# Attention scores computed twice, the second time with keys on partitions, and other products handed out between PSUM banks

## The chip, the cores and the metric

The kernel runs on one core of a Trainium2 chip. A core has five engines that each work through a queue of their own: TensorE (PE) for matrix products and transposes, VectorE (DVE), ScalarE (ACT) and GpSimd (POOL) for elementwise work, and SyncE (SP), which here issues the DMAs. The engines wait for one another through semaphores. The metric is the device time of one execution in microseconds (us). The kernel before took 1918.61 us as the median of 3 runs (1916.52 to 1922.07).

## What is computed

The input `x` is 4 sequences of 256 tokens with 512 channels in float32. Three layers follow one another: causal attention with an adapter, a feed-forward layer with clusters together with a state-space mixer, and the same feed-forward layer once more at the end. The change concerns the attention and the order in which the first feed-forward layer is worked off beside it. The part of the reference that matters:

```python
qkv = jnp.einsum('btc,oc->bto', x, w_attn)
q, k, v = jnp.split(qkv, 3, axis=-1)          # 32 heads of 16 channels, rotated
scores = jnp.einsum('bhqd,bhkd->bhqk', q, k) / jnp.sqrt(hd)
scores = jnp.where(causal, scores, -jnp.inf)
attn = jax.nn.softmax(scores, axis=-1)
y = jnp.einsum('bhqk,bhkd->bhqd', attn, v)
...
ascores = jnp.einsum('bhqd,xhkd->bhqk', q, ak) / jnp.sqrt(C)   # 10 adapter positions
ascores = gating[0] * jax.nn.softmax(ascores, axis=-1)
y = y + jnp.einsum('bhqk,xhkd->bhqd', ascores, av)
return jnp.einsum('btc,oc->bto', y, w_proj)
```

## The kernel before

The kernel is written for a framework that hands out tiles from pools and orders the instructions itself: each engine's queue is made by a list scheduler from the order in which the code asks for the work, from the dependences and from the buffers that a pool has. So the queues of PE, DVE, ACT, POOL and SP need not follow the source line by line; where this matters, the order of the built program is told. A pool with n buffers lets the n+1st tile begin only when the first has been read. PSUM, where PE writes, has eight banks; the attention's pools hold 2 (`ps`), 3 (`ps_s`), 2 (`ps_t`) and 1 (`ps_y`) of them.

Exact float32 products are made of three products of rounded parts (`mm3`, lines 106 to 114): high with high, high with low, low with high. A 512x512 projection of 128 tokens is 12 matmuls in this form.

Attention goes over 4 batches b, and in a batch over 8 units u of 4 heads. Two units share one set of turned pieces (q, 8 heads):

- `prepared(b)`: normalization, transposes, projections to queries, keys and values (`projected`), rotation on DVE and POOL.
- `pieces(b, q)`: a head's 16 channels are stacked as high, high, low parts and one slot of zeros, 64 rows in all (`stacked`: an ACT cast at L305, a POOL subtraction at L306), and turned by PE (`trp`, L380), so that one product over 64 rows gives an exact score. The first head of a pair lies in rows 0 to 63, the second in rows 64 to 127.
- `scores(b, u)`: queries on partitions. Score products (`sc`, L425), the causal mask added by a product with a constant (L429), the row maximum on DVE (L434), the exponential on ACT for each head with the row sum accumulated (L437).
- `turn`: the exponentials are transposed by PE (`ptr`, L452), three groups of four per unit, and copied from PSUM by DVE and ACT (L453).
- `weigh`: the product with the values (`py`, L462 and L468), four heads in the four 32-column groups. `gathered`: transposed back (`try`, L479), divided by the row sum (L484, L485).
- `adapter_scores` (`pa` L390, `sa` L394, `tra` L397), once per q; `adapted(b)`: the adapter's softmax for all heads at once (L496 to L503), then `pt`, `paT` and `pya`.
- `closed` adds both parts and turns them (L527, L530); `ended` projects them (`po`) and adds to x (L543).
- `fed`: the first feed-forward layer for 128 tokens (`Feed.tile`, 24 products of 288 columns). Four tiles may start when the last batch begins, the others when their attention has ended.

The loop (L608) runs over units; in one iteration it asks for the scores of unit i, the transposes of i-1, the product with the values of i-2 and the gathering of i-3. At its end it takes one step of each generator in `jobs` (the next batch's `prepared`, the adapter) and two of `slow` (`fed`). A step there is a whole projection of 12 products, or a whole feed-forward tile.

The mixer follows from about 392 us on. The change does not touch it.

Of the kernel before, what the change touches and what calls it, by code (L numbers as in the profile page):

```python
# [9 lines left out]
F32 = mybir.dt.float32  # L10
# [67 lines left out]
def hybrid_kernel(  # L78
# [36 lines left out]

    def warmed(o, vs):

        for v in vs:
            nc.tensor.matmul(o[:, : v.shape[1]], ones, v, start=True, stop=True)
# [52 lines left out]
    class Feed:  # L172
# [23 lines left out]
        def tile(self, t, xs, halves):  # L196

            p2 = self.p2
            pa, pb = halves
            for j, o in enumerate(halves):  # L200
                mm3(o, [[v[:, k, :] for v in xs] for k in range(KC)],
                    [[v[:, k, j, :] for v in self.w] for k in range(KC)])
# [29 lines left out]
    def attention(later):  # L232
        with ExitStack() as es:
# [6 lines left out]
            ps = pool("a_m", 2, space=PSUM)  # L240
            ps_s = pool("a_s", 3, space=PSUM)
            ps_t = pool("a_t", 2, space=PSUM)
# [25 lines left out]
            def projected(xs, w, where):  # L268
                pq = where[0].tile([P, C], F32, name="pq", tag=where[1])
                mm3(pq, [[v[:, k, :] for v in xs] for k in range(KC)],  # L270
                    [[v[:, k, :] for v in w] for k in range(KC)])
                return pq
# [20 lines left out]
            stacks = [[w1.tile([P, 8, 4, HD], F32R, name=f"st{f}{i}") for i in range(NS)] for f in range(2)]  # L293
            for f in range(2):
                for v in stacks[f]:
                    nc.gpsimd.memset(v.bitcast(F32), 0.0)
# [4 lines left out]
            def stacked(src, f, n=P):  # L301
                st = stacks[f][turn_at[f] % NS]
                turn_at[f] += 1
                v = src.unsqueeze(2)
                nc.scalar.copy(st[:n, :, HI[f], :], v.to_broadcast([n, 8, 2, HD]))  # L305
                nc.gpsimd.tensor_tensor(  # L306
                    st[:n, :, LO[f], :], src, st[:n, :, 0, :].bitcast(F32), ALU.subtract
                )
                return st.rearrange("p h s d -> p (h s d)")
# [9 lines left out]
            def adapter_weights():  # L319
# [9 lines left out]
                for q in range(4):  # L329
                    s = stacked(ak[:20, q * 8 : q * 8 + 8, :], 1, 20)  # L330
# [20 lines left out]
            vs = [w1.tile([P, 2, C + HD], F32, name=f"av{i}") for i in range(2)]  # L351
            for v in vs:
                nc.gpsimd.memset(v[:, :, C:], 0.0)

            qk, turned_ = {}, {}

            def prepared(b):
# [3 lines left out]
                for c in range(2):  # L361
                    xs.append(normed(norm, 2 * b + c))
                    yield
                    for f, w in ((0, wq_s), (1, wk_s)):
                        qk[b, c, f] = rotated(projected(xs[c], w, where), c, f, f"r{f}{c}")
                        yield
                for c in range(2):
                    nc.scalar.copy(vs[b % 2][:, c, :C], projected(xs[c], wv_s, where))
                    yield

            def pieces(b, q):

                out = []
                for f in range(2):
                    o = p2.tile([P, 4, L], F32R, name=f"pc{f}", tag=f"pc{f}")
                    for c in range(2):
# [5 lines left out]
                        nc.scalar.copy(o[:, :, cs], tr) if f else nc.vector.tensor_copy(o[:, :, cs], tr)  # L382
                    out.append(o)
                turned_[b, q] = out
# [17 lines left out]
            state = {}  # L402

            def begin(b):
                state[b] = {
                    "as": p2.tile([P, 2, NH, NA], F32, name="as"),
                    "rs": p2.tile([P, 2, NH], F32, name="rs"),
# [5 lines left out]
            def scores(b, u):  # L413

                qT, kT = turned_[b, u // 2]
                rs = state[b]["rs"]
                es_ = [p2.tile([P, 4, (c + 1) * P], F32, name=f"e{c}", tag=f"e{c}") for c in range(2)]
                for c in range(2):
                    n = (c + 1) * P
                    for pr in range(2):  # L420
                        rows = slice(64 * pr, 64 * pr + 64)
                        sc = ps_s.tile([P, 2, L], F32, name="sc", tag="sc")
                        for j in range(2):
                            blk = (u % 2) * 2 + j
                            nc.tensor.matmul(  # L425
                                sc[:, j, :], qT[rows, blk, c * P : (c + 1) * P], kT[rows, blk, :],
                                start=(j == 0), stop=False,
                            )
                        nc.tensor.matmul(  # L429
                            sc[:, :, n - P : n], identb, negb.unsqueeze(1).to_broadcast([P, 2, P]),  # L430
                            start=False, stop=True,
                        )
                        nm = p3.tile([P, 2], F32, name="nmx", tag="nmx")
                        nc.vector.tensor_reduce(nm, sc[:, :, :n], AX.X, ALU.max, negate=True)  # L434
                        for j in range(2):
                            h = 4 * u + 2 * j + pr
                            nc.scalar.activation(  # L437
                                es_[c][:, 2 * j + pr, :], sc[:, j, :n], AF.Exp,
                                bias=nm[:, j : j + 1], accum_out=rs[:, c, h : h + 1],
                            )  # L440
                return es_

            def turn(es_):
                e0, e1 = (
                    p2.tile([P, 4, (2 - c) * P], F32, name=f"eT{c}", tag=f"eT{c}") for c in range(2)
                )
                for src, k, dst in (
                    (es_[0], 0, e0[:, :, :P]), (es_[1], 0, e0[:, :, P:]), (es_[1], 1, e1)
                ):
                    pt = ps_t.tile([P, 4, P], F32, name="ptr", tag="pt")  # L450
                    for j in range(4):
                        nc.tensor.transpose(pt[:, j, :], src[:, j, k * P : (k + 1) * P], ident)  # L452
                    nc.scalar.copy(dst, pt) if k else nc.vector.tensor_copy(dst, pt)  # L453
                return e0, e1

            def weigh(b, u, eT):

                v = vs[b % 2]
                py = ps_y.tile([P, L], F32, name="py", tag="py")
                for j in range(4):  # L460
                    h = 4 * u + j
                    nc.tensor.matmul(  # L462
                        py[32 * j : 32 * j + 32, :], v[:, 0, h * HD : h * HD + 32], eT[0][:, j, :],
                        start=True, stop=False,
                    )
                for j in range(4):
                    h = 4 * u + j
                    nc.tensor.matmul(  # L468
                        py[32 * j : 32 * j + 32, P:], v[:, 1, h * HD : h * HD + 32], eT[1][:, j, :],
                        start=False, stop=True,  # L470
                    )
                ys = p2.tile([P, L], F32, name="ys")
                nc.scalar.copy(ys, py)
                return ys

            def gathered(b, u, ys):
                tr = ps.tile([P, 2, 4, 32], F32, name="try", tag="m")
                for c in range(2):
                    nc.tensor.transpose(  # L479
                        tr[:, c].rearrange("p h d -> p (h d)"), ys[:, c * P : (c + 1) * P], ident  # L480
                    )
                st = state[b]
                ry = p2.tile([P, 2, 4], F32, name="ry")
                nc.vector.reciprocal(ry, st["rs"][:, :, 4 * u : 4 * u + 4])  # L484
                nc.vector.tensor_tensor(  # L485
                    st["y"][:, :, 64 * u : 64 * u + 64].rearrange("p c (h d) -> p c h d", h=4),
                    tr[:, :, :, :HD], ry.unsqueeze(3).to_broadcast([P, 2, 4, HD]), ALU.mult,
# [45 lines left out]
            def ended(b):  # L533
                st = state.pop(b)
                pos = []
                for c in range(2):
                    pos.append(ps.tile([P, C], F32, name="po", tag="m"))
                    cs = slice(c * P, (c + 1) * P)
                    mm3(pos[c], [[v[:, k, cs] for v in st["yT"]] for k in range(KC)],
                        [[v[:, k, :] for v in wp_s] for k in range(KC)])  # L540
                for c, po in enumerate(pos):
                    t = 2 * b + c
# [3 lines left out]
                    if feed is None:  # L546
                        continue
                    feed.norm.stats(t)
                    feed.norm.root(t, t + 1)
                    if b < B - 1:  # L550
                        slow.append(fed(feed, t))
                    else:
                        late[t] = p2.tile([P, C], F32, name="axn", tag="t1")
                        feed.norm.scale(t, late[t])
# [6 lines left out]
            def fed(f, t):  # L561
                xs = normed(f.norm, t)
                yield
                f.tile(t, xs, [ps.tile([P, FH], F32, name="pd", tag="m") for _ in range(2)])
# [40 lines left out]
            n = B * 8  # L605
            es_, eTs, yss = {}, {}, {}
            feed, late = None, {}
            for i in range(n + 3):  # L608
                if i < n:
                    b, u = divmod(i, 8)  # L610
                    if u == 0:
                        begin(b)
                        pieces(b, 0)
                        if i == 0:
                            jobs.append(adapter())
                        if b + 1 < B:
                            jobs.append(prepared(b + 1))
                    if u == 6:
                        jobs.append(adapted(b))
                    es_[i] = scores(b, u)  # L620
                    if u % 2 == 0 and i > 0:
                        adapter_scores(b, u // 2)
                if 1 <= i <= n:
                    eTs[i - 1] = turn(es_.pop(i - 1))
                if 2 <= i <= n + 1:
# [584 lines left out]
```

## Time and profile before

| | before |
|---|---|
| median of 3 runs | 1918.61 us (1916.52 to 1922.07) |
| profiled execution, own time | 1916.66 us |
| its span, first to last instruction | 1914.9 us |
| PE busy | 1866.0 us, 97% |
| DVE, ACT, POOL busy | 77%, 72%, 19% |
| attention (with the first feed-forward mixed in) | about 0 to 392 us |
| first scores of batches 0, 1, 2, 3 | 36.06, 120.23, 202.3, 284.5 us |
| mean granted TensorE clock | 0.990 |

How to read a profile line: `L425 PE MATMUL sc<-pc,pc 64*128 64x256 f32 x128 | 32.7, 332 | 0.3 <-ACT e L437 0.3` is the group of matmuls from line 425 that write tiles named `sc` from two tiles named `pc`; the weights have 64 rows and 128 columns, the moving operand is 64x256. There are 128 of them, busy 32.7 us in all and 332 ns each on average, and PE sat idle for 0.3 us just before them, which an ACT instruction of line 437 ended. Matmuls are pipelined, so their records overlap: how long one really holds the engine is seen from start to start. In a timeline a line begins with the start and the duration in us. A table of stretches gives, after the stretch's length, the busy time and the number of instructions of PE, its weight loads, DVE, ACT and POOL, then the clock that TensorE was granted as a share of full speed, the DMA share and GB/s.

### The profile page before, as it was taken

The page shows a single profiled execution, that of the slowest core. Times are in us where ns is not written, and L with a number is a line of the kernel's source. Part 1 is how long each engine was busy: PE and PEld are TensorE (multiplying, and loading weights), DVE is VectorE, ACT ScalarE, POOL GpSimd, SP SyncE. Part 2 cuts the span into 40 slices and gives each one's busy share as a digit, 9 for nine tenths or more (in the row PEclk, how much of TensorE's full clock was granted, in tenths as well). Part 3 has the DMA queues.
Part 4 walks back from the last instruction along what each step waited for, and adds up shares of the span by engine and source line. Part 5 has one row for each costly group of instructions (what it writes and reads, how often), then busy time and mean ns, then how long its engine had stood idle before and what let it go on. Part 6 is the DMA issues. An engine that isn't in the chain of part 4 may idle for free.

```text
span 1914.9 us, 29954 instructions
## 1 busy us (share of the span) xinstructions
PE 1866.0 (97%) x10690; PEld 1468.9 (77%) x10690; DVE 1475.2 (77%) x2324; ACT 1383.2 (72%) x2873; POOL 361.0 (19%) x308
## 2 busy tenths in 40 slices
PE   7999999989999999999999999999999999999997
PEld 6767767767777787888787878877777788787786
DVE  5556657678998777877877797778777877877777
ACT  5665667557898677876787787778677877786753
POOL 4212120011331111222111121212111211131100
PEclk7999999989999999999999999999999999999999
DMA  4000000014455554544455454446454554455341
GB/s 141 1 1 1 1 21 24 12 38 155 169 192 184 160 168 140 160 154 160 149 164 161 149 172 156 148 147 187 149 165 154 160 159 160 138 166 162 119 123 49
DMA packets 151909, 240.35 MB, mean 126 GB/s; under 512 B 12368, under 2 KB 77520, under 8 KB 151760
## 3 DMA queue, kind: packets, MB, share of 16 engines
q1 hardware_dynamic: 151760, 238.44, 39.1%
q8 instruction: 84, 1.38, 0.3%
q14 instruction: 65, 0.53, 0.1%
HBM read 202.75 MB, written 35.65 MB: 124 GB/s over the span
## 4 chain that ended last, share of the span: by engine, by line
PE 84%; DVE 6%; ACT 4%; DMA 2%; issue 1%; SPq 0%; DVEq 0%; ACTq 0%
PE pp L112 12%; PE pp L113 11%; PE pp L114 11%; PE pyy L928 8%; PE pog L112 6%; PE pog L114 6%; PE pog L113 6%; PE sc L425 3%; PE trx L913 3%; PE ptr L452 2%; DVE acc L854 2%; PE py L462 1%; PE sc L429 1%; PE trp L380 1%; DMA wor<-in_wout_dram 1%
## 5 line engine op out<-in xcount | busy, mean ns | idle before, releaser
L112 PE MATMUL pp<-mx,w 128*128 128x512 f32 (+1 forms) x1160 | 465.6, 401 | 8.4 <-DVE acc L854 7.9
L114 PE MATMUL pp<-mx,w 128*128 128x512 f32 (+1 forms) x1160 | 454.2, 392 | 0.0
L113 PE MATMUL pp<-mx,w 128*128 128x512 f32 (+1 forms) x1160 | 454.2, 392 | 0.0
L854 DVE SCALAR_TENSOR_TENSOR acc<-pp,cw_s,acc 128x1012 f32<-128x1012 f32 (+2 forms) x240 | 304.8, 1270 | 23.1 <-ACT acc L847 22.4
L902 DVE TENSOR_TENSOR em<-em,gm 128x1536 f32<-128x1536 f32 x128 | 228.4, 1785 | 94.3 <-ACT em L896 86.0
L112 PEld LDWEIGHTS pp<-mx,w 128*128 128x128 f32 x1160 | 218.6, 188 | 66.0 <-issue 9.9
L114 PEld LDWEIGHTS pp<-mx,w 128*128 128x128 f32 x1160 | 218.5, 188 | 45.5 <-issue 0.4
L113 PEld LDWEIGHTS pp<-mx,w 128*128 128x128 f32 x1160 | 218.9, 189 | 40.7 <-issue 0.7
L890 POOL TENSOR_SCALAR_AFFINE_SELECT r<-r 128x512 f32<-128x512 f32 x128 | 144.6, 1129 | 526.6 <-DMA r<-cumd 418.5
L951 POOL TENSOR_TENSOR sq<-sq,acc 128x1024 f32<-128x1024 f32 x55 | 132.6, 2410 | 581.8 <-ACT acc L950 581.8
L104 ACT CAST w<-wr 128x512 fp32r<-128x512 f32 x144 | 88.5, 615 | 187.6 <-PE pp L113 164.4
L112 PE MATMUL pog<-wo,gh 128*128 128x512 f32 x512 | 204.3, 399 | 0.0
L114 PE MATMUL pog<-wo,gh 128*128 128x512 f32 x512 | 200.3, 392 | 0.0
L113 PE MATMUL pog<-wo,gh 128*128 128x512 f32 x512 | 199.9, 390 | 0.0
L895 ACT ACTIVATE em<-r,col_t 128x128 f32<-128x128 f32 x512 | 165.0, 391 | 48.2 <-PE pyy L928 46.5
L928 PE MATMUL pyy<-em,xd 128*64 128x256 f32 (+1 forms) x2048 | 189.1, 330 | 2.4 <-DVE em L902 2.4
L928 PEld LDWEIGHTS pyy<-em,xd 128*64 128x64 f32 x2048 | 134.2, 137 | 63.6 <-issue 21.7
L898 ACT ACTIVATE em<-r,col_t 128x128 f32<-128x128 f32 x512 | 166.5, 389 | 0.0
L886 DVE TENSOR_SCALAR em<-r,col_t 128x128 f32<-128x128 f32 x512 | 137.1, 327 | 12.1 <-PE pyy L928 10.1
L914 DVE TENSOR_TENSOR xd<-trx,dt_t 128x512 f32<-128x512 f32 x128 | 86.2, 683 | 54.6 <-PE trx L913 54.4
L105 DVE TENSOR_TENSOR w<-wr,w 128x512 fp32r<-128x512 f32 x139 | 97.4, 702 | 37.8 <-ACT w L104 37.3
L437 ACT ACTIVATE e<-sc,nmx 128x128 f32<-128x128 f32 (+1 forms) x256 | 105.2, 424 | 15.0 <-DVE nmx L434 14.9
(287 smaller groups left out, 3313.4 us busy)
## 6 DMA issues: line engine op xcount, KB each, us to landing
wr<-in_win_dram SPq DMA_DIRECT2D x287, 256.0 KB, 2.8
r<-cumd SPq DMA_DIRECT2D x128, 512.0 KB, 4.1
spill<-gb SPq DMA_DIRECT2D x63, 512.0 KB, 2.8
gr<-spill SPq DMA_DIRECT2D x120, 256.0 KB, 3.5
wor<-in_wout_dram SPq DMA_DIRECT2D x64, 256.0 KB, 3.1
out_dram<-x SPq DMA_DIRECT2D x8, 256.0 KB, 2.3
x<-in_x_dram SPq DMA_DIRECT2D x1, 1536.0 KB, 10.2
gr<-spill SPq DMA_DIRECT2D x8, 192.0 KB, 2.5
```

What stands on the lines that cost most here:

```text
L112: nc.tensor.matmul(o, lh, rh, start=(first and k == 0), stop=False)
L113: nc.tensor.matmul(o, lh, rl, start=False, stop=False)
L114: nc.tensor.matmul(o, ll, rh, start=False, stop=(last and k == n - 1))
L437: nc.scalar.activation(es_[c][:, 2 * j + pr, :], sc[:, j, :n], AF.Exp, bias=nm[:, j : j + 1], accum_out=rs[:, c, h : h + 1],)
L854: nc.vector.scalar_tensor_tensor(av[:, :, d:], pv[:, :, : L - d], cw_s[:, ch, tap : tap + 1], av[:, :, d:], ALU.mult, ALU.add,)
L886: nc.vector.tensor_scalar(e[:, b, 2, :], rv[:, b, 1, :], col_t[:, h, b, 1:2], 0.0, ALU.subtract, ALU.min,)
L890: nc.gpsimd.affine_select(rv[:, :, 0, :], rv[:, :, 0, :], pattern=[[0, B], [1, P]], compare_op=ALU.is_ge, fill=-1e30, base=0, channel_mult ...
L895: nc.scalar.activation(e[:, b, 1, :], rv[:, b, 1, :], AF.Exp, bias=col_t[:, h, b, 2:3])
L898: nc.scalar.activation(e[:, b, 0, :], rv[:, b, 0, :], AF.Exp, bias=col_t[:, h, b, 0:1])
L902: nc.vector.tensor_tensor(e, e, gm, ALU.mult)
L928: nc.tensor.matmul(py[d, b, k * P :], xd[:, 2 * b + k, d], es2[hh][:, b, 2 * k : 2 if k == 0 else 3, :].rearrange("p s i -> p (s i)"), sta ...
L951: (nc.gpsimd if n < NB - 1 else nc.vector).tensor_tensor(sq, sq, x2, ALU.add)
```

## The change

- The scores are computed twice. `tops(b, q)`, for 8 heads at once, has queries on partitions as before and takes only the row maximum; its score products alternate between the two 64-row groups, which write two banks, and the first 128 queries are paired with the first 128 keys only. The negated maxima are turned by PE (`trm`), copied by ACT (`mT`) and put by two small DMAs into the fourth slot of the turned queries, rows 48 and 112. `numerators(b, q)`, one iteration later, computes the scores with keys on partitions; ones in the fourth slot of the keys make the negated maximum a term of the same product. ACT takes the exponential of whole banks of 512, without a bias and without a row sum. The causal mask on the diagonal blocks is set by two `affine_select` on POOL.
- `turn` goes: its 24 transposes and 6 copies per q. `weigh` takes the exponentials as they are. The values have a column of ones behind each head, so the row sum comes out as a 17th column, and `gathered` takes its reciprocal from PSUM, for 8 heads at once.
- PSUM: `ps` has 3 banks, `ps_s` 4, `ps_y` 1; `ps_t` goes.
- The loop runs over q (16 and 2 more). Projections, the po products and the feed-forward tiles give way after every three products (`mm3_steps`). `aside(k)` takes k such steps from `jobs`, in strict order, or else from `slow`; the loop calls it between the banks of `tops` and `numerators` and in `pieces` (`drained`).
- `adapted(b)` and `ended(b)` are put first in `jobs` at q = 3; `prepared(b + 1)` is completed before the next batch's first pieces. The adapter's own keys use the stacks of the queries, since those of the keys now hold ones.

The diff, cut to its core:

```diff
+    def mm3_steps(o, ls, rs):
+        n = len(ls)
+        for k in range(n):
+            mm3(o, ls[k : k + 1], rs[k : k + 1], k == 0, k == n - 1)
+            if k < n - 1:
+                yield
...
-            ps = pool("a_m", 2, space=PSUM)
-            ps_s = pool("a_s", 3, space=PSUM)
-            ps_t = pool("a_t", 2, space=PSUM)
+            ps = pool("a_m", 3, space=PSUM)
+            ps_s = pool("a_s", 4, space=PSUM)
...
+            VW = HD + 1
+            vs = [w1.tile([P, 2, NH * VW + HD], F32, name=f"av{i}") for i in range(2)]
             for v in vs:
-                nc.gpsimd.memset(v[:, :, C:], 0.0)
+                nc.gpsimd.memset(v, 1.0)
+            for v in stacks[1]:
+                nc.gpsimd.memset(v[:, :, 3, 0:1].bitcast(F32), 1.0)
...
-            def scores(b, u):
...
-            def turn(es_):
...
+            def tops(b, q):
+                qT, kT = turned_[b, q]
+                nm = p2.tile([P, 2, NMW], F32, name="nmx", tag="nmx")
+                def banks(parts):
+                    made = []
+                    for c, js in parts:
+                        n = (c + 1) * P
+                        pair = [
+                            ps_s.tile([P, len(js), n], F32, name="sc", tag="sc") for _ in range(2)
+                        ]
+                        for i, j in enumerate(js):
+                            for pr in range(2):
+                                rows = slice(64 * pr, 64 * pr + 64)
+                                nc.tensor.matmul(
+                                    pair[pr][:, i, :], qT[rows, j, c * P : (c + 1) * P], kT[rows, j, :n],
+                                    start=(i == 0), stop=False,
+                                )
+                        made += [(c, js, pr, sc) for pr, sc in enumerate(pair)]
+                    for c, js, pr, sc in made:
...
+                        at = pr * 4 + js[0]
+                        nc.vector.tensor_reduce(
+                            nm[:, c, at : at + len(js)], sc, AX.X, ALU.max, negate=True
+                        )
+                banks([(1, (0, 1))])
+                yield
+                banks([(1, (2, 3))])
+                yield
+                banks([(0, (0, 1, 2, 3))])
+                yield
+                tr = ps.tile([NMW, 2, P], F32, name="trm", tag="m")
+                for c in range(2):
+                    nc.tensor.transpose(tr[:, c, :], nm[:, c, :], ident)
+                mT = p2.tile([8, 2, P], F32R, name="mT", tag="mT")
+                nc.scalar.copy(mT, tr[:8])
+                for pr in range(2):
+                    load(
+                        qT[64 * pr + 48 : 64 * pr + 49].bitcast(F32),
+                        mT[4 * pr : 4 * pr + 4].rearrange("p c i -> p (c i)").bitcast(F32),
+                    )
+            def numerators(b, q):
...
+                                pair[pr][:, i, :], kT[rows, j, k * P : (k + 1) * P], qT[rows, j, k * P :],
...
+                        nc.scalar.activation(to, sc, AF.Exp)
+                banks(0, (0, 1))
+                yield
+                banks(0, (2, 3))
+                yield
+                banks(1, (0, 1, 2, 3))
+                for pr in range(2):
+                    v = e[pr][:, 0:2].rearrange("p s j i -> p (s j) i")
+                    nc.gpsimd.affine_select(
+                        v, v, pattern=[[0, 8], [1, P]],
+                        compare_op=ALU.is_ge, fill=0.0, base=0, channel_multiplier=-1,
                     )
...
+                nc.vector.reciprocal(ry.unsqueeze(3), tv[:, :, :, HD : HD + 1])
...
+            def aside(k):
+                for _ in range(k):
+                    while jobs + slow:
+                        of = jobs if jobs else slow
+                        if next(of[0], 0) == 0:
+                            of.pop(0)
+                            continue
+                        break
...
+            for i in range(n + 2):
...
+                next(top, 0)
+                aside(2)
+                next(wgh, 0)
+                aside(1)
+                next(wgh, 0)
+                aside(1)
+                next(num, 0)
+                aside(1)
+                next(top, 0)
...
+                if 0 < i < n:
+                    adapter_scores(b, q)
+                    if q == 3:
+                        jobs.insert(0, adapted(b))
+                if 2 <= i:
+                    bq = divmod(i - 2, 4)
+                    gathered(*bq)
...
+                    if bq[1] == 3:
+                        closed(bq[0], 3)
+                        jobs.insert(0, ended(bq[0]))
+                aside(1)
+                if i + 1 < n:
+                    if (i + 1) % 4 == 0:
+                        while (i + 1) // 4 not in ready:
+                            aside(1)
+                    drained(pieces(*divmod(i + 1, 4)), 1)
+                    aside(1)
```

## The prediction

> **What bounds the kernel now.** I read the page's engine shares and its chain first, then busy time by stretches, then the engine timelines inside attention, then single rows for prices.
>
> ```profile
> PE 1866.0 (97%) x10690; PEld 1468.9 (77%) x10690; DVE 1475.2 (77%) x2324; ACT 1383.2 (72%) x2873; POOL 361.0 (19%) x308
> PE 84%; DVE 6%; ACT 4%; DMA 2%; issue 1%; SPq 0%; DVEq 0%; ACTq 0%
> ```
>
> TensorE (PE) is the bound, also in attention, by stretches (start and end; length; PE, weight loads, DVE, ACT, POOL busy; granted clock):
>
> ```profile
> 30.00:35.00 5.00, 2.38 (x20) 1.90 (x19) 3.85 (x6) 2.54 (x7) 4.55 (x6) 1.00 0.00 2
> 35.00:40.00 5.00, 4.98 (x24) 3.54 (x23) 2.21 (x5) 4.51 (x14) 1.32 (x3) 0.50 0.01 2
> 40.00:45.00 5.00, 4.50 (x20) 3.01 (x18) 1.96 (x5) 2.43 (x10) 0.00 (x0) 0.50 0.00 0
> 110.00:150.00 40.00, 39.84 (x281) 29.02 (x274) 24.03 (x52) 26.58 (x94) 4.86 (x9) 1.00 0.01 2
> 150.00:190.00 40.00, 39.89 (x270) 28.30 (x269) 25.46 (x54) 24.12 (x89) 8.78 (x13) 1.00 0.00 1
> ```
>
> PE is never free once attention runs; DVE and ACT are busy 60 to 66%. The first rows show the other thing to remember: after 2.6 us without matmuls in 5, the clock is 0.50 for the next ten. How long a product really holds PE is in the distances between starts:
>
> ```profile
> 160.17 0.50 PE L425 MATMUL sc<-pc,pc 64*128 64x256 f32 x2
> 160.60 0.28 PE L429 MATMUL sc<-negb,identb 128*128 128x256 bf16 x1
> 161.08 0.72 PE L390 MATMUL pa<-pc,akbd 128*80 128x256 f32 x4
> 161.63 1.04 PE L452 MATMUL ptr<-con,e 128*128 128x128 f32 x8
> 163.35 0.64 PE L462 MATMUL py<-eT,av 128*32 128x256 f32 x8
> 163.81 0.39 PE L468 MATMUL py<-eT,av 128*32 128x128 f32 x4
> 170.53 0.39 PE L112 MATMUL pq<-wq,axs 128*128 128x512 f32 x1
> 170.77 0.39 PE L113 MATMUL pq<-wq,axs 128*128 128x512 f32 x1
> ```
>
> A score product of 64 rows: 0.43 for two, 0.215 each. Four pa: 0.55. Transposes: about 0.11 each, and some 0.1 where the kind of product changes. Eight py in four column groups: 0.46, so 0.06 each, though 256 wide: groups run beside each other. A projection: 0.235.
>
> **What it removes and adds on PE.** Per q (8 heads) before: 16 scores 3.4, 8 masks 1.3, 24 transposes of exponentials 3.0, py 1.55, pa 0.55, tra 0.2, try 0.45, 16 trp 1.6: 12.0 us. After: the transposes go; there are 16 score products (half of them 128 wide, for the causal width) and 16 more with keys on partitions. They alternate between the two 64-row groups and write two banks. No row shows this form. It costs at most 0.215 each as above, and at least what the py column groups show, a pair in the time of one. I take the pair (eight pairs at 0.21, eight at 0.11, masks 1.1, changes of kind 0.5: 4.2) since py is the nearest row; the other end adds 3.0. With trm 0.25 and the unchanged py, pa, tra, try and trp it is 8.7. A batch also has 72 projections and 24 po (22.6) and some 4.5 of other transposes and adapter products. So PE's work falls from 75 to 62 us per batch. The first scores of batches 0 and 3 stand at 36.06 and 284.5 us, so a batch takes 82.8: 8 us of it are gaps and slow clock, under records that overlap.
>
> By "TensorEngine Tiling (Array Packing)", Overview and Gotcha 1, 64-row products can share the array when they write different PSUM banks, which is what the new form does; no run yet shows it.
>
> **Other engines.** Per q ACT loses 16 short exponentials, each with an accumulator read (0.45 and 0.34 from start to start, 6.3), and two copies of 0.59, and gets six 128x512 exponentials at 0.62 (the mixer's row L896) and one small copy: about 3.5 us less. DVE loses four copies of 682 ns. Neither bounds, so I give this nothing. POOL gets two affine selects of 128x1024 per q, SP two small DMAs per q (32 in all, 0.35 to 0.45 us to issue; SP's queue is nearly empty in attention).
>
> **What it makes PE wait for.** PE takes its products in order. In the changed program as built, py of a q stands right behind trm, then pa, tra, try and the four trp groups, then the first scores of the next q. Three projection products stand between banks only where some are left: 21, 39 and 36 (po among them) in three iterations of a batch, none in the fourth. The rows that price these waits, in groups by shape:
>
> ```profile
> L437 ACT ACTIVATE e<-sc,nmx 128x256 f32<-128x256 f32 x66 | 30.9, 478 | 4.7 <-DVE nmx L434 4.6
> L434 DVE TENSOR_REDUCE nmx<-sc 128x2 f32<-128x512 f32 x33 | 22.7, 687 | 10.0 <-PE sc L429 7.5 <-ACT e L437 1.6 <-ACT paT L513 0.6
> L382 DVE CAST pc<-trp 128x512 fp32r<-128x512 f32 x16 | 10.9, 686 | 3.0 <-PE trp L380 3.0
> L394 ACT COPY sa<-pa 80x256 f32<-80x256 f32 x8 | 2.9, 368 | 9.7 <-PE pa L390 9.7
> ```
>
> ```profile
> L890 POOL TENSOR_SCALAR_AFFINE_SELECT r<-r x128: 624/707/4776, 449.7 to 1801.8; 128x512 f32<-128x512 f32 x128
> ```
>
> Let S be the start of a q's last bank of second scores (0.5 us). An iteration without filler, with 0.1 to 0.25 per hand-over:
> - two exponentials, to S+2.0; two selects on POOL. The mixer's 128x512 select (the line above: shortest, median, longest) has a mean of 1129 ns; twice the shortest and the mean for 1024 is 1.22 to 2.3, and I take 1.22, for POOL has little else here. py ends at S+5.55 instead of S+2.4.
> - beside it the maximum: two reduces (0.69 each) to S+1.5, trm, a copy, two DMAs. Small ones in this trace land 2.4 to 3.1 us after issue, so S+5.2 to 5.6: hidden by py, just. pa to 6.15; sa 0.37 makes tra wait to 6.9; try to 7.55.
> - four trp groups, each waiting for a bank or a stack, 0.68 and 0.59 per evacuation: to 9.5. The next scores wait for the last evacuation: S+10.3.
> - three rounds of scores, masks, second scores on four banks, each waiting for a reduce of 0.69 or an exponential of 0.62 of the round before: 5.1 for 4.2 of work. End at S+15.4.
>
> So 15.4 us for 8.7 of work. The iterations with 39 and 36 filler products (9.2 and 8.5 us) come out by the same steps at 25.1 and 21.9 for some 19 and 17 of work, as the filler lies under part of the waits.
>
> The fourth is dearer, since the adapter's softmax is now queued earlier. pt stands in PE's order behind the first trp group, and this chain is ahead of it (DVE's and POOL's timelines):
>
> ```profile
> 102.72 0.81 DVE L496 TENSOR_REDUCE anm<-as 128x64 f32<-128x640 f32 x1
> 105.70 0.82 DVE L500 TENSOR_REDUCE asum<-as 128x64 f32<-128x640 f32 x1 [2.07 <-ACT as L498]
> ```
>
> ```profile
> 103.60 1.29 POOL L497 TENSOR_TENSOR as<-as,anm 128x640 f32<-128x640 f32 x1 [5.37 <-DVE anm L496]
> 107.89 1.29 POOL L503 TENSOR_TENSOR as<-as,asum 128x640 f32<-128x640 f32 x1 [2.58 <-DVE asum L502]
> ```
>
> From 102.72 to the end of POOL's L503 at 107.89 + 1.29 it takes 6.46 us; before, pt came at 113.88, long after. Now `as` is ready at S+7.4, pt at S+14, and PE stood free from about S+8.2: 5.8 us idle. Then pt, copy, pya, pt, copy, pya in turn cost 1.6 more. Period 29.9 for 16.5 to 17 of work.
>
> **Sum.** 15.4 + 25.1 + 21.9 + 29.9 = 92.3 us per batch, against 82.8: 9.5 more, 28.5 over three periods. The start has nothing yet to hand out (+3). The last batch and its tail (107.5 us before) has 144 feed-forward products of 0.13 as filler, 18.9 us, so I give its waits 0 to +7, and take 3.5. That is 35. My walk adds every hand-over in full; a tenth off four batches' 30 us of gaps is 12 less. The clock: the wait for pt is longer than the 2.6 us that were followed by clock 0.50, and ten us at half cost five if PE is full in them, nothing if it waits anyway; I take 1.5 a batch, 6 in all. 35 - 12 + 6 = 29 more. Against the profiled execution of 1916.7 (span 1914.9 and 1.8 around it), which lies 0.1% under the median, this is 1945, and 1946 against the median of 1918.6. The mixer's products and their order are untouched: zero, the cover being that PE fills 97% there anyway.
>
> "TensorE: Matmul & The Clock Gate", Part 1, has the clock fall to half after an idle window of about 3.4 us. The trace's 2.6 us in five is a little shorter and fell too. By the page one fall per batch would cost about 3.4 us of PE at half speed, an estimate of 1.7 each, 7 in all: about the same sum, and it speaks against the change.
>
> **Rivals.**
> - PE stays filled. If hand-overs are much shorter, and filler and py cover the rest, gaps stay at the 8 us per batch of before: 62 + 8 = 70 for 82.8, so -38, and -8 in the last batch: 1872. For it: PE bounds, and 13 us of its work per batch go. Against: one iteration in four has no filler. This is the case on the other side; it decides from gaps below 21 us per batch.
> - Both sides balance: gaps of 18 to 24, 1905 to 1930.
> - The 64-row pairs do not run beside each other: 3.0 more per q, partly in waits; 2 us by 16 q is +32, about 1978. For it: two score products of one row group follow at 0.215 though 256 wide, as pa is at 0.12. Against: the column groups.
> - Selects at 2.3: 2.2 more per q on the path of py, some of it under pa's DMA: +20 to 30, about 1970.
>
> **How the numbers follow.** The likeliest case (gaps of 25 to 34 us) 0.44, range 1930 to 1965; the pairs 0.08, the selects 0.08: both slower. PE filled 0.28, all of it faster. Balance 0.12: of it 0.04 faster, 0.04 within 0.3% and 0.04 slower (0.3% is about what a measurement of this kernel can tell from no change). So faster 0.32, same 0.04, slower 0.64. The range leaves a tenth on each side: 1866 to 1976.
>
> **What would show it.** Right: the first scores of batches 0 and 3 some 277 us apart instead of 248; PE waits named exponentials or POOL before py, DMA before pa, POOL before pt (about 5.8 us, once a batch); granted clock under 1 somewhere between 60 and 280. The steps on PE's work: starts of a new score pair 0.2 apart or less per pair, and PE's waits summing to about 25 us per batch. Wrong: periods of 70 us with PE waits under 10 per batch, or py never waiting for POOL.

## The result, and the profile after

The changed kernel takes 1985.9 us (median of 4 runs, 1983.1 to 1988.5) against 1918.6: 1.035 times as long, 95% interval 1.033 to 1.037. The forecast was slower, by 27 us (1946); it is 67, outside the range of 1866 to 1976. The profiled execution took 1988.5 us, span 1986.8, 71.9 more than the span of before. On the page, the engines and the chain that ended last:

```profile
PE 1867.6 (94%) x10562; PEld 1460.8 (74%) x10562; DVE 1437.5 (72%) x2196; ACT 1320.7 (66%) x2427; POOL 384.8 (19%) x342
...
PE 78%; ACT 7%; DVE 7%; DMA 3%; issue 2%; POOL 2%; SPq 0%; ACTq 0%; DVEq 0%; POOLq 0%
```

PE executes fewer products and is busy as long as before; POOL has come into the chain with 2%, and DMA has 3% where it had 2%. From the first scores of a batch to those of the next (last line: to the mixer's first product), columns as explained above the prediction, first before, then after:

```profile
36.10:120.20 84.10, 83.44 (x534) 58.51 (x534) 45.24 (x90) 52.48 (x191) 16.61 (x26) 0.93 0.00 1
120.20:202.30 82.10, 81.82 (x564) 58.42 (x561) 50.11 (x106) 52.18 (x190) 14.85 (x22) 1.00 0.00 1
202.30:284.50 82.20, 81.44 (x563) 57.83 (x560) 50.31 (x108) 54.97 (x193) 14.99 (x23) 1.00 0.04 13
284.50:403.70 119.20, 109.02 (x769) 81.31 (x766) 85.58 (x217) 71.13 (x231) 11.06 (x18) 0.99 0.08 23
```

```profile
36.80:131.00 94.20, 77.52 (x483) 52.99 (x482) 33.90 (x60) 34.19 (x76) 23.60 (x33) 0.80 0.00 1
131.00:229.70 98.70, 80.03 (x531) 54.44 (x530) 39.15 (x74) 35.86 (x77) 23.48 (x30) 0.83 0.00 1
229.70:332.20 102.50, 81.60 (x527) 55.07 (x526) 41.87 (x80) 40.98 (x85) 23.95 (x31) 0.82 0.05 16
332.20:474.80 142.60, 116.10 (x760) 85.19 (x760) 74.66 (x179) 57.92 (x121) 22.86 (x29) 0.84 0.06 15
```

Each batch is 10 to 20 us longer, the last stretch 23.4; the mixer, from 403.7 or 474.8 to the end, differs by 0.8. So all of it lies in the attention. Two things stand in these lines: gaps of 17 to 21 us in PE's busy time of a batch, where there were under 1, and a clock of 0.80 to 0.84 where it was 0.93 to 1.00. The gaps have names in the waits of PE (in all, times, longest):

```profile
PE py L540 <- POOL e L526: 19.8, 18, 4.1
PE pt L586 <- POOL as L580: 17.4, 3, 5.8
PE try L607 <- DVE y L604: 12.6, 8, 2.4
PE tra L428 <- ACT sa L425: 7.4, 15, 0.5
```

An iteration without filler, on PE's timeline:

```profile
88.38 0.64 PE L483 MATMUL trm<-con,nmx 128*72 128x128 f32 x2
90.30 3.83 PE L540 MATMUL py<-e,av 128*32 128x256 f32 x32 [1.28 <-POOL e L526]
94.06 1.14 PE L421 MATMUL pa<-pc,akbd 128*80 128x256 f32 x4
95.72 0.53 PE L428 MATMUL tra<-con,sa 80*128 80x80 f32 x2 [0.51 <-ACT sa L425]
96.03 1.06 PE L555 MATMUL try<-con,ys 128*128 128x128 f32 x4
96.75 2.50 PE L407 MATMUL trp<-con,st 128*128 128x128 f32 x16
100.18 0.50 PE L459 MATMUL sc<-pc,pc 64*128 64x256 f32 x4 [0.93 <-ACT pc L409]
100.62 0.39 PE L466 MATMUL sc<-negb,identb 128*128 128x256 bf16 x2
```

This is the serial row that the prediction walked through: trm, wait, py, pa, wait, tra, try, trp, wait, scores. py takes 3.8 us here and not 1.55, mostly since the clock is at half, and for a part since its third product starts only when POOL's second select has ended, at 91.30. The last two lines price the pairs: four score products of 256 columns in 0.44 us.

### The profile page after: what moved, and what is told of

Its sections match the earlier page's. It is cut to its first block, busy times and chain, and to the rows that moved or that the text cites. A ratio compares the mean times of both kernels' runs of the same rounds, so it can differ in the third digit from the quotient of the medians.

```text
span 1986.8 us, 29098 instructions
## 1 busy us (share of the span) xinstructions
PE 1867.6 (94%) x10562; PEld 1460.8 (74%) x10562; DVE 1437.5 (72%) x2196; ACT 1320.7 (66%) x2427; POOL 384.8 (19%) x342
## 4 chain that ended last, share of the span: by engine, by line
PE 78%; ACT 7%; DVE 7%; DMA 3%; issue 2%; POOL 2%; SPq 0%; ACTq 0%; DVEq 0%; POOLq 0%
PE pp L112 11%; PE pp L113 11%; PE pp L114 11%; PE pyy L1032 8%; PE pog L112 6%; PE pog L114 6%; PE pog L113 6%; PE trx L1017 3%; PE py L540 2%; PE sc L459 1%; DVE acc L958 1%; DMA wor<-in_wout_dram 1%; PE st L505 1%; PE pq L112 1%; PE sc L466 1%
## 5 line engine op out<-in xcount | busy, mean ns | idle before, releaser
L994 POOL TENSOR_SCALAR_AFFINE_SELECT r<-r 128x512 f32<-128x512 f32 x128 | 129.9, 1015 | 545.4 <-DMA r<-cumd 449.8
L990 DVE TENSOR_SCALAR em<-r,col_t 128x128 f32<-128x128 f32 x512 | 137.2, 327 | 11.8 <-PE pyy L1032 10.1
L105 DVE TENSOR_TENSOR w<-wr,w 128x512 fp32r<-128x512 f32 x139 | 98.7, 711 | 36.8 <-ACT w L104 36.5
L114 PEld LDWEIGHTS pog<-wo,gh 128*128 128x128 f32 x512 | 96.2, 188 | 21.1 <-issue 0.2
```

The costliest lines, as they stand in the source:

```text
L105: engine.tensor_tensor(hl[1], v, hl[0].bitcast(F32), ALU.subtract)
L114: nc.tensor.matmul(o, ll, rh, start=False, stop=(last and k == n - 1))
L990: nc.vector.tensor_scalar(e[:, b, 2, :], rv[:, b, 1, :], col_t[:, h, b, 1:2], 0.0, ALU.subtract, ALU.min,)
L994: nc.gpsimd.affine_select(rv[:, :, 0, :], rv[:, :, 0, :], pattern=[[0, B], [1, P]], compare_op=ALU.is_ge, fill=-1e30, base=0, channel_mult ...
```

## The experiments

Two theories stood at first. **W**: the waits, in the order of PE's queue, set the time, and a slow clock only fills time that would be waited anyway. **C**: the half clock that follows the waits costs most of the 67 us. Times are set against the 1985.9 us of the changed kernel; ratios are to the kernel before, on the same chip.

**Idle products in every gap** (changed kernel; `py` may be the bank of the next py)

```diff
+ def warm(o, k, n=P):
+     for _ in range(k):
+         nc.tensor.matmul(o.rearrange("p a b -> p (a b)"), con[:, :n], wp_s[0][:, 0, :], start=True, stop=True)
...
+ warm(py, 5)            # ahead of each py
+ warm(pt, 20, 80)       # ahead of the first pt
+ if banked and not jobs + slow: warm(banked[0], 2)   # in aside
```

> The changed kernel with every wait left in place, and idle products put into the gaps: 512-wide products of the identity with a projection weight into the bank of the next py, five asked for ahead of each py, two wherever nothing is left to hand out, twenty ahead of the first pt of a batch. Their results are overwritten. They add work and remove nothing. Theory C (the clock): in the profile after, PE is busy 77.5 to 81.6 us per batch at a granted clock of 0.80 to 0.83, where the sum of its work at full clock is 62; so most of the 67 us lost is half clock. Then the clock rises to above 0.97 and the time falls, to 1930 to 1955 us. Theory W (the waits themselves set the end, and a slow clock only fills time that would be waited anyway): the clock rises and the time does not fall, 1980 to 2005 us.

2005.3 us, the upper end of W; ratio 1.045 (1.043 to 1.047). The mean clock rose from 0.957 to 0.979. But 289 products of at least 0.235 us, 68 us of work, are more than the gaps hold, and those in py's bank brought a wait of their own for ys (9.0 us). This tells little of the clock, only that filling gaps with work costs as much as it fills.

**pt later**

```diff
-                        jobs.insert(0, adapted(b))
+                        held.append(adapted(b))
+                        next(held[0])
...
                 next(top, 0)
+                if held:
+                    jobs.insert(0, held.pop())
                 aside(1)
```

> The changed kernel with the adapter's softmax started at the same place, but pt and pya handed out in the middle of the next iteration, so that PE no longer stands 5.8 us in front of pt. W: the wait of 17.4 us and some 1.5 us a batch of serial copies go, 1962 to 1968 us. C: the half clock that follows the wait for some 20 us a batch goes too, 1945 to 1960 us, and the stretches at half clock around 105 to 135, 200 to 237 and 300 to 367 us become shorter.

1959.1 us (ratio to before 1.022, 1.018 to 1.025): 27 less than the changed kernel. That lies a microsecond inside C's range and 3 below W's, and the four runs spread from 1955.0 to 1971.0, so it does not decide. The iteration with pt fell from 30.8 to 19.0 us, while the next one rose from 26.2 to 28.8.

**The mask as a product**

```diff
+                    for sc in pair:
+                        nc.tensor.matmul(sc[:, :, :P], negb,
+                            identb.unsqueeze(1).to_broadcast([P, len(js), P]), start=False, stop=True)
...
-                    nc.gpsimd.affine_select(v, v, pattern=[[0, 8], [1, P]],
-                        compare_op=ALU.is_ge, fill=0.0, base=0, channel_multiplier=-1)
```

> The changed kernel with the causal mask of the second scores added by a product with the same constant (six more per q, 0.12 to 0.23 us each, some 1 us per q) in place of the two selects on POOL, 1.09 us each and 2.2 in a row. PE's wait for POOL before py (19.8 us) goes to a wait of at most a few us for ACT. W: 20 less waits, 16 more work, within 10 us of the changed kernel, 1975 to 1990. C: the same, and a further gain only if the clock rises; more PE work in the bare iterations keeps it up, 1955 to 1975.

1985.6 us: nothing. PE's waits in this run show why:

```profile
PE pt L585 <- POOL as L579: 18.5, 4, 5.8
PE pa L421 <- DMA pc<-mT: 14.2, 12, 1.8
...
PE py L539 <- ACT e L521: 2.4, 3, 1.2
```

POOL's 19.8 us are gone, and 14.2 us for the two small DMAs have taken their place: pa reads the whole tile of turned queries, into whose fourth slot the DMAs write, and they land just after py. A bare iteration of this run has py end at 90.85, and then:

```profile
92.49 0.67 PE L421 MATMUL pa<-pc,akbd 128*80 128x256 f32 x4 [1.63 <-DMA pc<-mT]
```

**Both**

> Both edits together: pt later and the mask as a product. W: the sum of the two, 1955 to 1965 us. C: less than the sum, since fewer iterations reach the low clock at all, 1920 to 1945 us.

1965.8 us (1.022, 1.017 to 1.026; the runs spread from 1951.6 to 1971.5): a microsecond above W's range, and no better than pt alone. The DMA's wait stayed (12.4).

**Idle products ahead of pt alone** (the twenty of the first run, nothing else)

> The changed kernel with idle products in one place only: twenty 512-wide products (4.7 us at full clock) into pt's bank, ahead of the first pt of a batch, where PE stands idle for 5.8 us in each of three batches. They add nothing to the path as long as they end before POOL does. W (the waits set the end): no change, 1980 to 1992 us. C (half clock after that wait costs what it delays): the stretches at half clock after pt, 20 us and more in the profile after, go or shorten, and the time falls to 1955 to 1975 us.

1984.8 us: no change beyond noise. The wait in front of pt itself shrank from 17.4 to 4.0 us by hidden work, and half clock fell only from 157 to 132 us of the attention. Against C as it was put.

**The adapter's scores early, the mask as a product**

```diff
                 next(top, 0)
+                if 0 < i < n:
+                    adapter_scores(b, q)
+                    if q == 3:
+                        held.append(adapted(b))
+                        next(held[0])
                 aside(2)
...
-                if 0 < i < n:
-                    adapter_scores(b, q)
-                    if q == 3:
-                        jobs.insert(0, adapted(b))
+                if held:
+                    jobs.insert(0, held.pop())
```

(and the edit for the mask above)

> The changed kernel with the mask of the second scores as a product, and the adapter's scores asked for right after the first bank of first scores, so that pa does not stand behind the two small DMAs and tra does not stand between trm and the next pieces; the adapter's softmax starts there too. Nothing is left out. W: the waits for the DMAs (14 us), for sa (7), in front of pt (18 with the copies behind it) and for POOL (20) go: 40 to 55 us under the changed kernel, 1930 to 1945 us. C: with fewer waits the clock stays up as well, mean over 0.975 and 1895 to 1930 us. Rival: other waits take their place (trp for a bank or a stack, the next scores for the last copy), 1955 to 1975 us.

1885.4 us, ratio to before 0.982 (0.979 to 0.985): 100 us less than the changed kernel, and 33 less than the kernel before. All three expectations were too modest. In stretches of 40 us:

```profile
60.00:100.00 40.00, 39.28 (x306) 25.34 (x305) 18.80 (x33) 21.50 (x44) 8.50 (x14) 1.00 0.01 2
100.00:140.00 40.00, 38.57 (x295) 27.20 (x292) 21.51 (x43) 18.78 (x41) 10.04 (x13) 1.00 0.01 1
140.00:180.00 40.00, 39.38 (x333) 26.29 (x331) 20.44 (x38) 21.41 (x46) 6.72 (x11) 1.00 0.01 2
```

PE is filled, at full clock; batches take 72.7 to 75.9 us.

**One part alone in the kernel before: pairs of row groups**

```diff
-                    for pr in range(2):
-                        sc = ps_s.tile([P, 2, L], F32, name="sc", tag="sc")
-                        for j in range(2):
+                    pair = [ps_s.tile([P, 2, L], F32, name="sc", tag="sc") for _ in range(2)]
+                    for j in range(2):
+                        for pr, sc in enumerate(pair):
```

> The kernel before with one part of the change alone: its score products alternate between the two 64-row groups, into two banks at once. In the profile after, starts within such a pair are 0.003 to 0.004 us apart and pairs 0.21, against 0.215 for each product before; 256 products save some 27 us of PE's time. W (PE's work bounds before): 1893 to 1905 us. Rival: with three banks a pair waits for two of them, and DVE's and ACT's round sets the time instead, 1912 to 1925 us.

1901.6 us, 0.991 (0.989 to 0.992): 17 less, inside W's range, though 27 us of PE's time had been counted. Not every pair stays together in the queue that the scheduler makes: from 120 to 280 us a score product takes 0.182 us from start to start on average, 0.220 before.

**The same with the causal width** (`kT[rows, blk, :n]`, banks of `[P, 2, n]`)

> The same, and the first 128 queries are paired with the first 128 keys only, as in the changed kernel (the other 128 are masked anyway and were not read). 128 products of 256 columns become 128: another 6 to 7 us of PE's time. W: 1886 to 1900 us. Rival: as for the run before, within 3 us of it.

1907.7 us, 0.994 (0.992 to 0.996): outside both ranges. The narrower products bring no gain over the pairs alone, and the median is 6 us worse; why stays open.

**Idle products where PE was seen to wait**

```diff
+                for _ in range(12):
+                    nc.tensor.matmul(pa, con[:, :AW], wp_s[0][:, 0, :L], start=True, stop=True)
...
+                        for _ in range(0 if jobs or slow else 1):   # ahead of each pair of banks
+                            nc.tensor.matmul(pair[0].rearrange("p j n -> p (j n)"), con, wp_s[0][:, 0, :], start=True, stop=True)
```

(and twenty ahead of pt)

> The changed kernel with idle products only where PE was seen to wait: twelve 256-wide ones (1.4 us) into pa's bank, which the queue places between trm and py, twenty ahead of the first pt, and one ahead of each pair of score banks where nothing is left to hand out. Every wait stays. Equal iterations of the runs so far that differ in clock alone give the price of a microsecond at half clock: 26.2 us with 5.8 at half against 24.7 with 0.8, 23.5 with 23.5 against 21.3 with 14.2, 30.8 with 21.5 against 29.5 with 16.3, so 0.25, from 0.13 to 0.41; 157 us stand at half clock in the attention of the changed kernel. C: if half of that goes, 20 us less, 1955 to 1972 us, and bare iterations at 16 to 17 us instead of 18 to 20. W: the clock rises and the time stays, 1980 to 1995 us.

1981.3 us, ratio to before 1.032 (1.030 to 1.034); W by the time. But the third iterations of the batches, which have 8 filler products at most, did what C said: 18.7, 17.5 and 19.8 us (13.7, 3.4 and 10.2 of them at half clock) became 15.6, 16.7 and 17.5, all three at full clock. The sum hides most of it: the six iterations with more filler went from 147.1 to 151.9 us together (the first from 24.7 to 28.6, others up or down), as the twelve products are added work there and 20.9 us instead of 15.3 fell to half clock. The three with pt stayed the same in sum.

**The adapter's scores early, selects kept on POOL** (the early edit without the mask's)

> The changed kernel with the adapter's scores and softmax asked for early, as in the run at 1885 us, but with the mask left to the selects on POOL. If the order of pa, tra and pt is what cost most: 1890 to 1915 us, py still waiting for POOL in the iterations without filler. If both were needed (as the mask alone gained nothing, since pa's DMA stood right behind): 1930 to 1955 us.

1893.6 us, 0.986 (0.984 to 0.987). The order is what cost; the mask, worth nothing alone, is worth 8 us more once pa is out of the way.

**Feed-forward handed out twice as fast**

```diff
-                for _ in range(k):
+                for _ in range(k if jobs else 2 * k):
```

> The changed kernel, handing out two steps of three products instead of one wherever only feed-forward tiles are left. Before the last score product, 72 of 192 feed-forward products were done in the profile after, 120 in that of before; the remaining 48 (6.3 us at full clock) lie behind the attention. If the last batch's extra 23 us come from there: 5 to 12 us faster, 1974 to 1981. If from the waits of the last batch alone: within 3 us of the changed kernel.

In the changed kernel 1986.3 us in the median, nothing, though the runs spread from 1979.8 to 1987.2.

> The version at 1885 us with the same handing out of two steps of feed-forward products. 5 to 10 us faster, 1875 to 1881 us; rival: its last batch has few waits left to fill, 1883 to 1888 us.

In the version with pa early 1886.5 us, the rival: nothing. The products moved from the tail, the last q's first scores to the mixer (65.2 to 54.8 us), into the iterations before it (17.2 and 18.2 to 21.6 and 22.5). The rate of handing out is not where the last batch lost its time.

**Idle products in the iterations without filler alone** (`range(0 if jobs or slow else 12)` at pa)

> As the run with idle products at pa, pt and the score banks, but at pa only where nothing is left to hand out. Every wait stays, and the iterations with filler get no added work. At the price seen between equal iterations (0.23 us per us at half clock in the bare ones) and with some 80 of 157 us at half clock gone: C: 15 to 25 us faster than the changed kernel, 1960 to 1971 us. W: less than 8 us faster, 1978 to 1988.

1978.4 us (1.030, 1.028 to 1.032), 7.5 less, by the time W. One batch of this run lies at full clock throughout and can be set against the same batch of the changed kernel, which stands above from 131.00 to 229.70:

```profile
126.10:217.10 91.00, 79.19 (x581) 54.05 (x580) 39.20 (x75) 35.71 (x78) 23.44 (x30) 1.00 0.01 1
```

In the prediction's own periods, from one q's last bank of second scores to the next's:

| period, us (of it at half clock) | changed kernel | this run | predicted |
|---|---|---|---|
| 39 filler products | 25.1 (3.4) | 24.4 (0) | 25.1 |
| 36 | 21.1 (0) | 21.8 (0) | 21.9 |
| none | 17.6 (6.9) | 15.6 (0) | 15.4 |
| 21, and the wait for pt | 36.5 (27.2) | 29.1 (0) | 29.9 |
| the four | 100.3 (37.5) | 90.8 (0) | 92.3 |

From the batch's first scores to the next batch's it is 98.7 us (33.8 at half clock) against 91.0 (0.1). So the clock costs 7.7 us in this batch, 0.23 us for each at half; by the table's periods it is 0.25. The gain did not last: in the last batch, with the clock low again for 45 of its iterations' 74 us, this run is 4.7 us longer than the changed kernel.

**The adapter's scores early, the softmax and pt where the change put them**

```diff
                 next(top, 0)
+                if 0 < i < n:
+                    adapter_scores(b, q)
                 aside(2)
...
-                if 0 < i < n:
-                    adapter_scores(b, q)
-                    if q == 3:
-                        jobs.insert(0, adapted(b))
+                if 0 < i < n and q == 3:
+                    jobs.insert(0, adapted(b))
```

> The changed kernel with the adapter's scores alone asked for after the first bank of first scores; the softmax, and pt with its wait, stay where the change put them. The early run gained 92 us against the changed kernel, putting pt later alone gained 27. If pa in front of try and trp is the larger part: 1905 to 1925 us, batches of 76 to 80 us, with a wait for pt of 2 to 6 us left in each. If pt is the larger part and both overlap: 1945 to 1965 us.

1897.5 us, 0.988 (0.987 to 0.990): 88 of the 92 us, from the place of one call, and below both ranges. No wait for pt is left either, since its softmax has its input earlier. PE's timeline of a bare iteration in this run:

```profile
87.91 0.64 PE L483 MATMUL trm<-con,nmx 128*72 128x128 f32 x2 [0.51 <-DVE nmx L471]
88.34 1.06 PE L555 MATMUL try<-con,ys 128*128 128x128 f32 x4
89.05 1.32 PE L407 MATMUL trp<-con,st 128*128 128x128 f32 x8
90.30 1.06 PE L540 MATMUL py<-e,av 128*32 128x256 f32 x2
91.30 1.26 PE L407 MATMUL trp<-con,st 128*128 128x128 f32 x8
92.48 1.08 PE L540 MATMUL py<-e,av 128*32 128x256 f32 x8
93.49 0.89 PE L421 MATMUL pa<-pc,akbd 128*80 128x256 f32 x4
94.31 0.41 PE L540 MATMUL py<-e,av 128*32 128x128 f32 x4
94.65 0.51 PE L459 MATMUL sc<-pc,pc 64*128 64x256 f32 x4
```

With pa gone from behind trm, try and trp follow at once and cover POOL and the DMAs; py itself has become filler between the trp groups and even behind the next scores. From trm to the next first scores it takes 6.7 us, at half clock for most of it, against 11.8 in the changed kernel, also at half clock for most of it.

## Why the prediction was right and wrong

**PE's work.** Right in its price: pairs at 0.22, not 0.43, so the rival that pairs don't run beside each other is excluded. The sums are short on both sides. The 8 us between 75 and 82.8 were read as gaps and slow clock, but two batches of before take 82.1 and 82.2 us at clock 1.00 with gaps of 0.3 and 0.8: there they were time in which PE was busy. Likewise a batch of the version at 1885 us takes 72.7 us at full clock with 1.8 idle, where 62 were counted; by the expectation's 1 us per q, some 4 of it are the mask's products. The forecast goes by the walk and not by these sums.

**The waits.** The walk holds: at full clock, in the run with idle products inside its waits, the four periods take 90.8 us against 92.3, and each is within 0.8 us of what was walked (the table above). The changed kernel itself shows the same where its clock is full: 24.1 us with 39 filler products in the next batch, 21.1 and 21.9 with 36. The places are right too: the wait for pt was given as 5.8 us and is 5.8, three times; py waits for POOL, tra for sa. The select was taken at 1.22 us and takes 1.09:

```profile
L526 POOL TENSOR_SCALAR_AFFINE_SELECT e<-e x32: 1092/1093/1541, 72.1 to 423.2; 128x1024 f32<-128x1024 f32 x32
```

so the rival with long selects is out. That the DMAs are "hidden by py, just" was right to the point: taking POOL out laid them bare. "PE stays filled" fell.

**The tenth off.** "My walk adds every hand-over in full; a tenth off four batches' 30 us of gaps is 12 less." This step had no row behind it. The full-clock batch leaves room for 1.5 us a batch, not 3, and at the clock that was granted there was nothing to take off.

**The clock.** "I take 1.5 a batch, 6 in all" is the term that failed most. In the profile after, 157 us between 36 us and the mixer's start lie at half clock, in fifteen stretches, against 16 before. I expected one fall per batch, behind pt. It fell in the bare iterations too, with no long wait in them: the fall at 85.6 us stands here, in steps of 2 us.

```profile
82.00:84.00 2.00, 1.76 (x11) 0.98 (x9) 1.58 (x3) 1.25 (x3) 0.22 (x1) 1.00 0.00 0
84.00:86.00 2.00, 1.49 (x13) 1.21 (x13) 1.03 (x2) 1.09 (x2) 0.00 (x0) 0.89 0.00 0
86.00:88.00 2.00, 2.00 (x12) 1.05 (x12) 0.99 (x2) 0.00 (x0) 0.00 (x0) 0.50 0.00 0
```

PE was busy 78% of the 3.4 us before it. Priced at full clock from one batch (91.0 - 82.8 = 8.2, three times 24.6), the three batches' 47.0 us more divide into 24.6 for waits and some 22 for the clock, where 19.5 and 4.5 had been taken. This split rests on one undisturbed batch of one run and is an estimate; the 110 us at half clock in these three batches, at 0.23 to 0.25 each, give 25 to 28 for the clock.

**The last batch.** "I give its waits 0 to +7, and take 3.5": less 3 for the tenth and with 1.5 for the clock, 2 us had been taken for this stretch, and it was 23.4. The filler that it counted on, 144 feed-forward products, was not there: 72 stood before the last score product, none of them in the batch's first iteration. 47 us of the stretch lie at half clock, 11 us at the price above; for the rest there are waits for POOL (8.2) and for DVE at try2 (6.8) in that stretch. Handing out faster put 141 products before the last score product and recovered nothing, so the cause of this part stays open. With 0.7 at the start and 0.8 in the mixer and after, 24.6 + 22.4 + 23.4 + 1.5 make the 71.9 of the spans.

So the forecast had the mechanism, its sign and the walk through the waits. The steps that failed are the clock, 6 us where the estimate comes to some 33 (22 in three batches, 11 in the last), the last batch's waits, 0.5 net where some 12 are left beside the clock, and the tenth off. They feed each other: waits lower the clock, and a lower clock lengthens the products behind them.

What it did not see is which of the waits mattered. It told of the DMAs, the selects and pt as separate prices. One call stood behind most of it: the adapter's scores read a tile that a DMA still writes, and in PE's queue try and trp, which need neither, stood behind them. With the call early, the other waits are covered. That the DMA's tile is the reason is not shown by itself: the move also takes tra's wait for sa (7.4 us) and the two `ps` buffers of pa and tra out of this place, and starts the softmax sooner, and pt later alone gave 27 us.

## What to carry to other kernels

In an in-order queue, look for the instruction that reads a tile whose last part arrives late, and at what stands behind it without needing that part: the place of the call that holds it was worth 88 us here, while taking the wait for POOL out of the product ahead of it was worth nothing. When waits are spread over a stage, price the clock from equal pieces at full and at half clock, not from the longest wait alone. Idle products to hold the clock are added work wherever they are longer than the wait; here they gained 7.5 us at best and cost 19 at worst.

## What the runs showed of the hardware

In the profile after, the stretches at half clock have lengths of 3.4, 6.8, 10.2, 13.7, 20.5 and 44.4 us, multiples of 3.41. The Trainium skill, "TensorE: Matmul & The Clock Gate", Part 1, has a window of that length, and the lengths agree; it has the clock fall after an idle window, and here only two of the twelve falls between 36 and 400 us follow an idle one (119.7 and 321.1, in the wait for pt). The others follow windows in which PE was busy 44 to 95%, for instance 44, 45, 75 and 78% before the falls at 150.4, 191.4, 201.6 and 85.6. Of the full-clock windows from 36 to 400 us with 80 to 95% busy, one in fifteen was followed by half clock, of the 27 busier ones none.

Four 64-row products into two banks start 0.003 to 0.004 us apart within a pair, so the two row groups do run beside each other, as the Trainium skill, "TensorEngine Tiling (Array Packing)", Overview, has it; each pair takes 0.22 us, where one product of the kernel before takes 0.22 by itself.
